# Silu against tanh for the expert tiles that run beside a selective scan, one Trainium2 core

## The chip, the core and the metric

The kernel runs on one core of a Trainium2 chip. A core has a matrix engine (TensorE, PE in the profile, with its weight loads as PEld), an elementwise engine (VectorE, DVE), an engine for activation functions (ScalarE, ACT), a third elementwise engine that here also starts the indirect transfers (GpSimd, POOL), and a queue that starts most of the other transfers (SyncE, SP). Each engine works through its own list of instructions strictly in order; they meet only in semaphores. An instruction that has to wait holds up everything behind it on its engine.

The metric is the device time of the whole program in microseconds (us), as the median of several executions. Profiles are of one execution each.

## The reference

The model is one Mamba block and one mixture of experts, each with a residual and a layer norm, over 4096 tokens of width 256 in float32. Cut to what matters:

```python
xz = x @ W_in.T;  x_in, z = split(xz)                  # 512 + 512 wide
u  = silu(causal_conv4(x_in) + b_conv)
dt = softplus(u @ W_dt.T + b_dt);  B, C = u @ W_B.T, u @ W_C.T
h[t] = exp(dt[t] * A) * h[t-1] + dt[t] * B[t] * u[t]   # 512 channels x 16 states
y[t] = sum_n h[t] * C[t]
x1 = layernorm(x + (y * silu(z)) @ W_out.T)

p = softmax(x1 @ router.T);  six best of 32 experts by p + bias, weights renormalised
gate, up = split(x1 @ gate_up[e].T)                    # 128 + 128, for each chosen expert e
routed = sum_e weight_e * ((silu(gate) * up) @ down[e].T)
shared = (silu(x1 @ sg.T) * (x1 @ su.T)) @ sd.T
out = layernorm(x1 + routed + shared)
```

The change touches `silu(gate) * up` of the routed experts, and only for about half of them.

## The kernel before

**Chunks and units.** The 4096 tokens are cut into eight chunks of 512. For each chunk and each of two halves of the channels, 16 states by two blocks of 128 channels are scanned: 64 units of 128 channels by 512 tokens a chunk, 512 in all. The loop over units (L1223) writes the instructions of all engines in program order. For unit q it issues

- on ScalarE `keep(q-1)` (L1159), which copies the last column of the state that unit q-1 has left, and `exp_at(q+2)` (L1132), the decay factors of the unit after next, into a tile `h` in PSUM that has three buffers. So the exponential for unit q+2 may start only when VectorE has done with unit q-1, and it has to be ready when VectorE comes to unit q+2;
- on GpSimd `du_at(q+4)` (L1121), the input term, four units ahead;
- on VectorE the scan itself (L1260), which reads `h` and `du` and writes `h`, and the product with C (L1267), which writes `hc`;
- on TensorE, three units later, the transposes (L1178) that sum `hc` over the states.

**What runs beside the scans.** Everything else is cut into Python generators, kept in a list `threads`; `step()` (L160), called once for each unit, advances each of them to its next `yield`, and whatever it issues takes its place in the engines' lists there. Nothing is moved afterwards. The generators are: `front(c+1)`, which projects, convolves and gates the next chunk and makes its step sizes (L867; its two long silu at L917 and L919, its logarithms at L971); `tail(c-1)` and `prepare`, which project the output of the chunk before, normalise it, route it and compute the shared expert (the square root of the norm at L181, a tanh for the shared gate at L367); `copies`, which scatter the routed rows into tiles of one expert each; and, from the third chunk on, the expert tiles.

**The expert tiles.** There are 224 tiles of 128 rows. They go in pairs. The 56 pairs of the first six chunks run as `pair` (L674) beside the scans of chunks 3 to 7, with weights loaded for them; the other 56 run as `through_all` (L1293) after the scans, with all experts' weights in SBUF. A `pair` waits for its rows, transposes them (L641), copies them back through ScalarE (L644, L647), multiplies with the gate and up weights into one PSUM bank `pg` (L682: gate in half 0, up in half 1), takes tanh of half the gate on ScalarE (L690), and one `yield` later, that is one unit later, makes `(tanh(g/2) + 1) * g` and its product with `up` on VectorE (L693, L694). Then come the down projection (L700), the weighting by ScalarE (L658) and an indirect add to memory by GpSimd (L664). `(tanh(g/2) + 1) * g` is twice silu(g); the row weights carry the factor one half.

**Function tables.** The profile shows the rows `ACT_TABLE_LOAD` on ScalarE, 1283 ns each, wherever the next function is not in the set that is loaded. The compiler places them directly ahead of the instruction that needs them. In the kernel before they stand ahead of the square root, the long silu, the logarithm, and ahead of the first exponential after each of these; none stands ahead of a tanh while exponentials run.

Of the kernel before, what the change touches and what calls it, by code (L numbers as in the profile page):

```python
# [10 lines left out]
AF = mybir.ActivationFunctionType  # L11
ALU = mybir.AluOpType
# [48 lines left out]
def kernel(  # L61
# [20 lines left out]
    nc = tc.nc  # L82
# [50 lines left out]
    def room():  # L133
        while held[0] >= len(pools):
            yield

    def bank(name):
        held[0] += 1
        turn[0] += 1
        return pools[turn[0] % len(pools)].tile([P, T], F32, tag="mm", name=name)  # L140

    def free():
        held[0] -= 1
# [4 lines left out]
    def take(tag, n):  # L148
        while live.get(tag, 0) >= n:
            yield  # L150
        live[tag] = live.get(tag, 0) + 1

    def give(tag):
        live[tag] -= 1
# [479 lines left out]
    def turned_rows(j, xt):  # L634
        yield from take("xsT", 2)
        yield from room()
        pt = bank(f"pt_{j}")
        pt4 = pt.rearrange("p (i k t) -> p i k t", i=2, k=KD)
        for i in range(2):
            for k in range(KD):  # L640
                nc.tensor.transpose(pt4[:, i, k, :], xt[:, i, ts(k, P)], ident)  # L641
        yield
        xT = q2.tile([P, 2, KD, P], F32, tag="xsT", name=f"xsT_{j}")
        nc.scalar.copy(xT.rearrange("p i k t -> p (i k t)"), pt)  # L644
        free()
        no = q2.tile([P, 2], I32, tag="no", name=f"no_{j}", bufs=8)
        nc.scalar.copy(no, xt[:, :, D])  # L647
        turned_out.add(j)
        yield
        return xT, no  # L650

    def added(j, po, wt, no, behind):

        tag, n = ("ytl", 4) if behind else ("yt", 2)
        yield from take(tag, n)
        yt = (f3 if behind else q2).tile([P, 2, D], F32, tag=tag, name=f"{tag}_{j}", bufs=n)
        for i in range(2):
            nc.scalar.mul(yt[:, i, :], po[:, i, :], wt[:, i : i + 1])  # L658
        free()
        yield  # L660
        for i in range(2):
            yield
            apart_from[0] = False
            a = nc.gpsimd.indirect_dma_start(  # L664
                out=acc[(j + i) % LANES],
                out_offset=bass.IndirectOffsetOnAxis(ap=no[:, i : i + 1], axis=0),
                in_=yt[:, i, :],
                in_offset=None,
                compute_op=ALU.add,
            )  # L670
            adds.append(a.ins)
        give(tag)

    def pair(j, xt, wt, gu, dn):  # L674

        xT, no = yield from turned_rows(j, xt)
        yield from room()
        pg = bank(f"pg_{j}").rearrange("p (h i t) -> p h i t", h=2, i=2)
        for h in range(2):
            for i in range(2):  # L680
                for k in range(KD):
                    nc.tensor.matmul(  # L682
                        pg[:, h, i, :], gu[i][:, k, ts(h, P)], xT[:, i, k, :],
                        start=(k == 0), stop=(k == KD - 1),
                    )
        give("xsT")
        yield from take("hm", 2)
        yield
        gt = q2.tile([P, 2, P], F32, tag="gt", name=f"gt_{j}")
        nc.scalar.activation(gt, pg[:, 0, :, :], AF.Tanh, scale=0.5)  # L690
        yield
        hm = q2.tile([P, 2, P], F32, tag="hm", name=f"hm_{j}")
        nc.vector.scalar_tensor_tensor(gt, gt, 1.0, pg[:, 0, :, :], ALU.add, ALU.mult)  # L693
        nc.vector.tensor_mul(hm, gt, pg[:, 1, :, :])  # L694
        free()
        yield
        yield from room()
        po = bank(f"po_{j}").rearrange("p (i d) -> p i d", i=2)
        for i in range(2):
            nc.tensor.matmul(po[:, i, :], hm[:, i, :], dn[i], start=True, stop=True)  # L700
        give("hm")
        give("dn")
        yield
        yield from added(j, po, wt, no, False)
# [713 lines left out]
```

## Time and profile before

| | |
|---|---|
| time, median of 3 executions | 1851.69 us (1851.32 to 1852.23) |
| the profiled execution: its time, its span | 1859.8 us, 1857.9 us |
| granted TensorE clock, mean | 0.839 |
| scans, first to last start | 72.0 to 1507.0 us |
| tanh of the pairs (L690), first to last start | 602.4 to 1524.3 us |
| PE, DVE, ACT, POOL busy over the span | 73%, 75%, 53%, 65% |
| ACT_TABLE_LOAD rows of the exponential's line L1132 | 29, 37.2 us |

The span runs from the first to the last instruction of the profiled execution. A group's row gives the source line, the engine, the operation, its output and inputs with their shapes, the number of instructions, then the busy time in us and the mean ns of one, then the idle time of the engine directly ahead of them and what ended it. A row of waits reads "who waited, for whom: total us, how many times, longest us". A row of the timeline gives the start in us, the duration in us, engine, line, operation, and in brackets the idle time ahead of it.

### The profile page before, as it was taken

What the parts mean: (1) busy time and instruction counts of PE and PEld (TensorE: products, weight loads), DVE (VectorE), ACT (ScalarE), POOL (GpSimd) and SP (SyncE); (2) the same over time, 40 slices, a digit from 0 to 9 for tenths busy, and PEclk for the clock granted to TensorE, in tenths of its full rate; (3) what the DMA queues carried; (4) which work ended last, traced back from release to release, by engine and by line L of the source; (5) the groups of instructions that cost most, each with busy time, mean ns of one, the idle gap of its engine ahead of it and who ended that gap; (6) DMA issues with size and microseconds to landing.
All of it is one profiled execution on the core that took longest, in us unless ns stands there. A gap on an engine that the chain in (4) does not pass through costs nothing. (4 is left out here: it accounts for less than half of the span.)

```text
span 1857.9 us, 24110 instructions
## 1 busy us (share of the span) xinstructions
PE 1359.2 (73%) x6208; PEld 944.8 (51%) x6208; DVE 1399.4 (75%) x2328; ACT 990.9 (53%) x2131; POOL 1216.3 (65%) x961
## 2 busy tenths in 40 slices
PE   8585696588669866986699668967775668699940
PEld 4242453355345545653566456645654566477730
DVE  1689989998998899779987998799979854122217
ACT  3676464547445755475557465756552333355533
POOL 0455644774585569665886599658956874878863
PEclk9796697779769887988989888988886987799975
DMA  8443692673469667875989589858998996599879
GB/s 238 136 126 102 219 307 77 164 212 123 94 192 257 166 160 177 251 206 126 258 215 263 131 234 245 236 139 214 271 257 236 260 268 100 123 145 144 144 131 306
DMA packets 318121, 355.40 MB, mean 191 GB/s; under 512 B 65056, under 2 KB 245024, under 8 KB 317984
## 3 DMA queue, kind: packets, MB, share of 16 engines
q1 hardware_dynamic: 274400, 296.02, 56.7%
q0 software_dynamic: 41472, 57.80, 17.3%
q8 instruction: 51, 0.84, 0.2%
q14 instruction: 86, 0.70, 0.1%
q10 hardware_dynamic: 2112, 0.05, 0.1%
HBM read 244.97 MB, written 108.77 MB: 190 GB/s over the span
## 5 line engine op out<-in xcount | busy, mean ns | idle before, releaser
L1121 POOL TENSOR_TENSOR du<-wall,bb 128x512 f32<-128x512 f32 x512 | 694.9, 1390 | 417.5 <-DVE h L1260 216.8
L1260 DVE TENSOR_TENSOR_SCAN h<-h,hlast,du 128x512 f32<-128x512 f32 x512 | 657.1, 1283 | 52.2 <-ACT hlast L1159 27.3
L1178 PE MATMUL y<-ident,hc 128*128 128x128 f32 x2048 | 345.2, 311 | 124.0 <-DVE hc L1267 104.0
L1132 ACT ACTIVATE h<-wall,aneg 128x512 f32<-128x512 f32 x512 | 353.7, 692 | 95.0 <-DVE hc L1267 80.4
L1267 DVE TENSOR_TENSOR hc<-h,cb 128x512 f32<-128x512 f32 x512 | 354.3, 692 | 58.6 <-DMA cb<-bcd 14.2
L1178 PEld LDWEIGHTS y<-ident,hc 128*128 128x128 f32 x2048 | 278.6, 162 | 233.9 <-DVE hc L1267 136.3
L552 POOL DMA_INDIRECT xs<-row,at x192 | 192.3, 1001 | 72.5 <-issue 39.2
L664 POOL DMA_INDIRECT acc<-ytl,no x112 | 174.8, 1561 | 59.4 <-issue 32.9
L664 POOL DMA_INDIRECT acc<-yt,no x112 | 177.5, 1585 | 53.2 <-ACT yt L658 28.7
L1159 ACT COPY hlast<-h 128x1 f32<-128x1 f32 x448 | 70.9, 158 | 260.7 <-DVE hc L1267 260.4
L1310 DVE SCALAR_TENSOR_TENSOR gt<-gt,pg 128x256 f32<-128x256 f32 x56 | 23.6, 421 | 175.5 <-ACT gt L1308 175.5
L682 PE MATMUL pg<-xsT,gu 128*128 128x128 f32 x896 | 123.8, 297 | 31.5 <-ACT xsT L644 25.4
L682 PEld LDWEIGHTS pg<-xsT,gu 128*128 128x128 f32 x896 | 118.0, 210 | 46.8 <-ACT xsT L644 29.5
L700 PE MATMUL po<-dn,hm 128*128 128x256 f32 x224 | 75.6, 469 | 83.5 <-DVE hm L694 35.6
L941 PE MATMUL pd<-wall 128*128 128x512 f32 x256 | 127.9, 649 | 9.5 <-DVE key L469 4.2
L905 PE MATMUL pv<-wall 128*128 128x512 f32 x256 | 117.4, 602 | 5.9 <-ACT hlast L1159 3.2
L1301 PE MATMUL pg<-wall,xsT 128*128 x448 | 113.0, 398 | 1.0 <-ACT xsT L644 1.0
L700 PEld LDWEIGHTS po<-dn,hm 128*128 128x128 f32 x224 | 46.9, 228 | 102.2 <-DVE hm L694 33.5
L641 PE MATMUL pt<-ident,xt 128*128 128x128 f32 x448 | 76.7, 298 | 24.1 <-DMA xt<-xs 21.2
L1301 PEld LDWEIGHTS pg<-wall,xsT 128*128 128x128 f32 x448 | 85.1, 200 | 12.3 <-ACT xsT L644 2.1
L941 PEld LDWEIGHTS pd<-wall 128*128 128x128 f32 x256 | 51.6, 211 | 66.8 <-issue 60.6
L641 PEld LDWEIGHTS pt<-ident,xt 128*128 128x128 f32 x448 | 61.0, 155 | 41.9 <-issue 25.3
(192 smaller groups left out, 1929.0 us busy)
## 6 DMA issues: line engine op xcount, KB each, us to landing
bb<-bcd SPq DMA_DIRECT2D x256, 256.0 KB
cb<-bcd SPq DMA_DIRECT2D x256, 256.0 KB
xs<-blank SPq DMA_DIRECT2D x55, 578.0 KB
xt<-xs SPq DMA_DIRECT2D x224, 128.5 KB
gu<-in_gate_up_t_dram SPq DMA_DIRECT2D x112, 256.0 KB
dn<-in_down_t_dram SPq DMA_DIRECT2D x112, 128.0 KB
wall<-acc SPq DMA_DIRECT2D x24, 512.0 KB
acc<-blank SPq DMA_DIRECT2D x16, 512.0 KB
```

The source lines that it names most:

```text
L552: i = nc.gpsimd.indirect_dma_start(out=xs, out_offset=bass.IndirectOffsetOnAxis(ap=at[:, b, k : k + 1], axis=0), in_=row[:, b, :], in_offs ...
L641: nc.tensor.transpose(pt4[:, i, k, :], xt[:, i, ts(k, P)], ident)
L664: a = nc.gpsimd.indirect_dma_start(out=acc[(j + i) % LANES], out_offset=bass.IndirectOffsetOnAxis(ap=no[:, i : i + 1], axis=0), in_=yt[:, ...
L682: nc.tensor.matmul(pg[:, h, i, :], gu[i][:, k, ts(h, P)], xT[:, i, k, :], start=(k == 0), stop=(k == KD - 1),)
L700: nc.tensor.matmul(po[:, i, :], hm[:, i, :], dn[i], start=True, stop=True)
L941: nc.tensor.matmul(pd, w_dt[:, k, ts(m, P)], u[:, k, :], start=(k == 0), stop=(k == M - 1),)
L1121: nc.gpsimd.tensor_mul(parts(q, du), u, row_for(q, 0))
L1132: nc.scalar.activation(h[:, ts(i, Tc)], dt_of[c][:, m + i, :], AF.Exp, scale=aneg[:, m + i, n : n + 1],)
L1178: nc.tensor.matmul(y_of[c, g][b // 2][:, b % 2, ts(m + j - 2 * g, P)], hc[:, ts(j * nb + b, P)], ident, start=(opens and j == 0 and b % 2 ...
L1260: nc.vector.tensor_tensor_scan(h, h, du_of.pop(q), hlast[:, n, m : m + 1], ALU.mult, ALU.add)
L1267: nc.vector.tensor_mul(parts(q, hc), parts(q, h), row_for(q, 1))
L1301: nc.tensor.matmul(pg[:, i].rearrange("p h t -> p (h t)"), xT[:, i, k, :], w, start=(k == 0), stop=(k == KD - 1),)
```

## The change

The gate's activation in `pair` becomes silu instead of tanh of the half, and the first of the two VectorE instructions goes. The second is now a three-operand instruction that multiplies silu by 2 and by `up`; the factor 2 keeps the row weights as they are. `through_all` and the shared expert keep the tanh.

```diff
         gt = q2.tile([P, 2, P], F32, tag="gt", name=f"gt_{j}")
-        nc.scalar.activation(gt, pg[:, 0, :, :], AF.Tanh, scale=0.5)
+        nc.scalar.activation(gt, pg[:, 0, :, :], AF.Silu)
         yield
         hm = q2.tile([P, 2, P], F32, tag="hm", name=f"hm_{j}")
-        nc.vector.scalar_tensor_tensor(gt, gt, 1.0, pg[:, 0, :, :], ALU.add, ALU.mult)
-        nc.vector.tensor_mul(hm, gt, pg[:, 1, :, :])
+
+        nc.vector.scalar_tensor_tensor(hm, gt, 2.0, pg[:, 1, :, :], ALU.mult, ALU.mult)
         free()
         yield
```

In the instruction lists of the two programs every engine keeps its order. VectorE has 56 instructions fewer. ScalarE has 107 more, all of them table loads: 54 ahead of the silu at L690, and 53 ahead of an exponential at L1132. The typical sequence on ScalarE was: exponential, tanh, `keep`, exponential. It is now: exponential, load, silu, `keep`, load, exponential.

## The prediction

> **What bounds the kernel now.** I read the page first, then the waits, then the timelines of ScalarE and VectorE around single tiles.
>
> ```profile
> span 1857.9 us, 24110 instructions
> ...
> PE 1359.2 (73%) x6208; PEld 944.8 (51%) x6208; DVE 1399.4 (75%) x2328; ACT 990.9 (53%) x2131; POOL 1216.3 (65%) x961
> ...
> L1260 DVE TENSOR_TENSOR_SCAN h<-h,hlast,du 128x512 f32<-128x512 f32 x512 | 657.1, 1283 | 52.2 <-ACT hlast L1159 27.3
> ...
> L1267 DVE TENSOR_TENSOR hc<-h,cb 128x512 f32<-128x512 f32 x512 | 354.3, 692 | 58.6 <-DMA cb<-bcd 14.2
> ```
>
> The scan and its product alone are 1011 us of VectorE, and they lie between 72 and 1510 us. In stretches of 180 to 190 us between 600 and 1330 us VectorE is busy for 156 to 167 us, 87 or 88%. So in the scans VectorE is the engine nearest to being the bound; what it still waits for there stands in the waits, columns total us, times, longest:
>
> ```profile
> DVE gt L693 <- ACT gt L690: 34.5, 15, 5.8
> DVE h L1260 <- ACT hlast L1159: 27.3, 14, 5.0
> DVE h L1260 <- ACT h L1132: 18.4, 14, 3.8
> ...
> DVE hc L1267 <- DMA cb<-bcd: 14.2, 8, 3.2
> ```
>
> The reader sees two things. The largest waits of VectorE in this part end at ScalarE: 34.5 us at the tiles' activation, 45.7 us at exponentials and `keep`. And ScalarE as a whole is not full: 106.2, 105.2, 108.2 and 111.6 us busy in four stretches of 180, 180, 180 and 190 us, 59%. So what counts is where on ScalarE the new work falls.
>
> **What a load costs.** One that is there already, with its neighbours on ScalarE:
>
> ```profile
> 895.83 0.15 ACT L1159 COPY hlast<-h 128x1 f32<-128x1 f32 x1
> 896.00 1.28 ACT L1132 ACT_TABLE_LOAD   x1
> 897.29 0.69 ACT L1132 ACTIVATE h<-wall,aneg 128x512 f32<-128x512 f32 x1
> ```
>
> It starts 0.02 us after the copy has ended, and the exponential starts 0.01 us after it: nothing beside the 1.283 us. Without a load the next instruction starts some 0.06 us before the last has ended (exponential to tanh below: 911.50 against 911.44), so I take 1.36 us for each load. 107 of them by 1.283 are 137 us of busy ScalarE; 43 of the 56 pairs lie between 600 and 1330 us, and take its share there from 59% to (431 + 86 x 1.283) / 730 = 74%.
>
> The Trainium skill, "ScalarE: Activation LUTs", section "What ACT_TABLE_LOAD costs", gives the same 1283 ns and adds a drain of about 1380 ns to every switch, 2.66 us in all; its rules say to do all of one table set before switching, which speaks against this change. No drain shows in the rows above. By the page a pair's two loads would put 5.3 us ahead of an exponential that has 3.7 us to spare, 1.6 us late for 54 pairs, an estimate of 87 us more; by the row they fit.
>
> **The change part by part.**
>
> *Removed: 56 instructions at L693.* The timeline of a pair in a quiet place, VectorE:
>
> ```profile
> 914.48 0.41 DVE L693 SCALAR_TENSOR_TENSOR gt<-gt,pg 128x256 f32<-128x256 f32 x1
> 914.92 0.42 DVE L694 TENSOR_TENSOR hm<-gt,pg 128x256 f32<-128x256 f32 x1
> ...
> 917.19 1.28 DVE L1260 TENSOR_TENSOR_SCAN h<-h,hlast,du 128x512 f32<-128x512 f32 x1
> ```
>
> From start to start one instruction is 0.44 us. The new form of L694 is that of the old L693 (414 against 421 ns, means over 56): no difference. 56 by 0.44 is 24.6 us, the upper end; the lower is 0. From it I take off: 7 pairs after 1442 us (3.1 us), because there the chain that ended last runs through transfers and GpSimd and not VectorE:
>
> ```profile
> 1442.64 11.78 DMA order<-li
> 1454.48 6.54 DMA bb<-bcd
> ```
>
> and 7 pairs in dense stretches (3.1 us, below), where VectorE would only wait longer for ScalarE. Of the 18.4 us left I let a fifth go at waits that VectorE does not set (matrix products for `pg`, `cb` transfers): 14.7 us.
>
> *Swapped: tanh for silu.* A silu over 2048 columns is 1911 ns, a tanh over 512 is 586 ns; the line through both gives 365 ns at 256 columns, the tanh here has 377. Nothing either way.
>
> *Added: a load ahead of silu.* ScalarE in the same place:
>
> ```profile
> 910.81 0.69 ACT L1132 ACTIVATE h<-wall,aneg 128x512 f32<-128x512 f32 x1
> 911.44 0.36 ACT L690 ACTIVATE gt<-pg 128x256 f32<-128x256 f32 x1
> 912.61 0.16 ACT L1159 COPY hlast<-h 128x1 f32<-128x1 f32 x1 [0.81 <-DVE hc L1267]
> 912.80 0.69 ACT L1132 ACTIVATE h<-wall,aneg 128x512 f32<-128x512 f32 x1
> ```
>
> The load waits for nothing, so where ScalarE stands idle for `pg` (16.2 us over 43 pairs) it is hidden in part; else silu ends 1.36 us later. Queued behind it on ScalarE are `keep` and the exponentials; waiting for it is L694, which stands one unit later on VectorE. I set the new end of each silu against the old start of its L693. Quiet pairs have room: 911.80 + 1.36 = 913.16, and VectorE comes at 914.48. Of 56 pairs 35 have it. 15 already make VectorE wait; there the delay is what the idle ScalarE does not hide, between 0 and 1.40 us, in sum 7.2. Another 6 lack 0.15 to 1.40 us, in sum 3.8. Together 11.0 us; bounds 0 and 56 x 1.36 = 76.
>
> *Added: a load ahead of the next exponential.* It stands behind `keep`, which waits for VectorE, so ScalarE's idle time before `keep` doesn't hide it (in chunk 7, without `keep`, it does). The exponential that ends at 913.49 is read at 917.19: 3.70 us to spare. Both loads take 2.72, and the removed instruction brings the scan 0.44 nearer: 0.5 us are left. That is the usual case; the middle value of this margin over the pairs is 3.7 us, but 12 of 53 have under 2.7. Following the delay down ScalarE's list until an idle stretch swallows it, 9 pairs make something on VectorE late: by 1.67, 1.83, 1.44, 0.46, 2.25, 1.35, 0.76, 2.58 and 0.24 us, 12.6 in sum. Most of them stand shortly ahead of the long silu, where ScalarE has no idle time and already makes a scan wait:
>
> ```profile
> 1196.88 1.28 ACT L917 ACT_TABLE_LOAD   x1
> 1198.17 1.91 ACT L917 ACTIVATE wall<-wall 128x2048 f32<-128x2048 f32 x1
> ...
> 1203.82 0.69 ACT L1132 ACTIVATE h<-wall,aneg 128x512 f32<-128x512 f32 x1
> ```
>
> ```profile
> 1204.61 1.29 DVE L1260 TENSOR_TENSOR_SCAN h<-h,hlast,du 128x512 f32<-128x512 f32 x1 [4.96 <-ACT hlast L1159]
> ```
>
> With the first part they overlap: counting the larger of the two for each pair gives 16.9 us, adding both 23.6. I take 20.3. From below it is bounded by 0 (the existing pairs of loads around the logarithms, such as that at 896.00, make no scan wait), from above by both loads of all 49 pairs before 1442 us, 133 us. I take a value near the low end, since it comes from the rows of the very places.
>
> *Behind.* Nothing moves on SP, GpSimd or TensorE. Late on ScalarE is also what follows silu: copies of rows (L644) for TensorE and `yt` (L658) for GpSimd's adds. GpSimd is four units ahead and already waits 216.8 us for VectorE at L1121, so up to 2.7 us are covered; without that cover the input terms would be late by as much. The end after 1510 us starts with loads that wait for the scans, so it shifts as a whole.
>
> **Sum:** 20.3 - 14.7 = 5.6 us slower. The profiled execution took 1859.8 us (span 1857.9), 8.1 over the median of 1851.7; I put the difference on the median: 1857.3 us.
>
> **Rivals.**
> *Faster: ScalarE's slack holds.* For it speaks the 41% of idle ScalarE, and the loads at the logarithms. If the added waits are the 11.0 us at L694 alone and 21 us of the saving land, it is 10 us faster, 1842. It decides as soon as the added waits stay under what lands of 24.6 us. Against it: the dense stretches have no idle time to give.
> *Nothing that can be measured:* waits and saving both near 15 to 18 us, 1852. For it speaks that the two sums are so near each other; measuring this kernel can tell about 0.2%, 3.7 us.
> *Much slower: delays spread.* My sums hold the other engines still. In the long chains of `front` ScalarE and TensorE wait for each other (ACT L910 for PE L905: 99.5 us), and a load there delays a copy, a product and the next copy, with exponentials queued behind them. If half of the second loads land, 25 x 1.36 = 34 us, with the 11.0, less 14.7: 30 us slower, 1882. Against it: 53 of these loads lie mostly in quiet stretches.
> *Silu next to the long silu would need no load:* excluded, the list has 54 loads for 56 silu.
>
> **How the numbers follow.** Forecast 0.45 (own range 1854 to 1866, a small part of it within 0.2%), faster 0.22, nothing 0.18, much slower 0.15. Slower is 0.42 + 0.15 = 0.57, within 0.2% is 0.18 + 0.03 = 0.21, faster 0.22. The range leaves out about half of the faster case below 1843, and most of the much slower above 1875.
>
> **What the profile will show.** ACT_TABLE_LOAD x54 at L690 and x82 at L1132, 1283 ns each with no gap; DVE 2272 instructions; the wait of L694 on silu from 34.5 to about 45 us; the scan's two waits on ScalarE from 45.7 to about 57; quiet pairs as before without waits. I am wrong if a load shows a gap behind it (a drain), if scans wait in quiet pairs, or if VectorE's waits on ScalarE grow by less than 12 us.

## The result and the profile after

The changed kernel takes 1867.68 us (median of 4 executions, 1865.91 to 1868.41) against 1851.96 us of the kernel before beside it: a ratio of 1.0075, 95% interval 1.0060 to 1.0091. By the ratio it is 14 us slower (11 to 17), by the two medians 16. The forecast was slower, by 5.6 us: the direction holds, the size does not.

The page of the profiled execution, and from the groups of ScalarE its table loads:

```profile
span 1866.2 us, 24155 instructions
...
PE 1361.1 (73%) x6208; PEld 945.7 (51%) x6208; DVE 1381.5 (74%) x2272; ACT 1125.0 (60%) x2238; POOL 1216.5 (65%) x961
```

```profile
L1132 ACT ACT_TABLE_LOAD x82 | 105.2, 1283 | 1.4
L690 ACT ACT_TABLE_LOAD x54 | 69.3, 1283 | 6.2 <-PE pg L682 5.2
```

VectorE has its 56 instructions fewer and is busy for 17.9 us less; ScalarE has 107 loads more and is busy for 134 us more. Against the columns of before (1399.4, 990.9) nothing else moved in the sums. The last scan ends at 1522.5 us after the span's start, before at 1508.3, 14.2 us later; so the loss lies in the scans. What comes after them took 343.7 us, before 349.6; over the profiled executions of all the kernels told here it takes 340 to 351 us, high and low without regard to the loads, and the profiled execution of the kernel before was itself 8 us over its median.

The waits of VectorE, columns as before (who, for whom: total us, times, longest):

```profile
DVE hm L694 <- ACT gt L690: 48.5, 24, 6.5
...
DVE h L1260 <- ACT hlast L1159: 33.9, 17, 6.2
DVE h L1260 <- ACT h L1132: 25.9, 20, 4.2
...
DVE h L1260 <- POOL du L1121: 12.9, 13, 2.3
```

The last of these rows in the kernel before:

```profile
DVE h L1260 <- POOL du L1121: 5.6, 6, 1.9
```

The wait for silu grew from 34.5 to 48.5 us (3.0 more are put down to `keep`), the scans' waits for ScalarE from 45.7 to 59.8, and the scans' wait for GpSimd's input terms from 5.6 to 12.9.

A pair shortly ahead of the long silu that the prediction showed. First VectorE in the kernel before, then ScalarE and VectorE in the changed one:

```profile
1188.90 0.42 DVE L693 SCALAR_TENSOR_TENSOR gt<-gt,pg 128x256 f32<-128x256 f32 x1 [0.48 <-ACT gt L690]
```

```profile
1200.26 1.28 ACT L690 ACT_TABLE_LOAD   x1
1201.55 0.38 ACT L690 ACTIVATE gt<-pg 128x256 f32<-128x256 f32 x1
1201.83 0.15 ACT L1159 COPY hlast<-h 128x1 f32<-128x1 f32 x1
1202.01 1.28 ACT L1132 ACT_TABLE_LOAD   x1
1203.30 0.69 ACT L1132 ACTIVATE h<-wall,aneg 128x512 f32<-128x512 f32 x1
```

```profile
1201.97 0.42 DVE L694 SCALAR_TENSOR_TENSOR hm<-gt,pg 128x256 f32<-128x256 f32 x1 [1.87 <-ACT gt L690]
...
1221.18 1.29 DVE L1260 TENSOR_TENSOR_SCAN h<-h,hlast,du 128x512 f32<-128x512 f32 x1 [6.16 <-ACT hlast L1159]
```

The product waits 1.87 us, 1.39 more than before (0.48); the prediction had 1.36 there. The scan that waited 4.96 us for the block with the long silu now waits 6.16. A pair in a quiet place, again ScalarE and VectorE:

```profile
918.87 1.28 ACT L690 ACT_TABLE_LOAD   x1
920.17 0.38 ACT L690 ACTIVATE gt<-pg 128x256 f32<-128x256 f32 x1
920.45 0.15 ACT L1159 COPY hlast<-h 128x1 f32<-128x1 f32 x1
920.62 1.28 ACT L1132 ACT_TABLE_LOAD   x1
921.91 0.69 ACT L1132 ACTIVATE h<-wall,aneg 128x512 f32<-128x512 f32 x1
```

```profile
921.83 0.41 DVE L694 SCALAR_TENSOR_TENSOR hm<-gt,pg 128x256 f32<-128x256 f32 x1
922.16 1.28 DVE L1260 TENSOR_TENSOR_SCAN h<-h,hlast,du 128x512 f32<-128x512 f32 x1
```

Neither instruction of VectorE has a bracket: both loads are covered. In the rows of both pairs the next instruction follows a load 0.01 us later, and so it does behind 161 of the 173 loads of this kernel; behind the other 12 stands an instruction that waits for another engine. There is no drain.

So the loads behave as read. What has to be explained is why the sum came out two and a half to three times as large.

### The profile page after: what moved, and what is told of

Its sections match the earlier page's. It is cut to its first block, busy times and chain, and to the rows that moved or that the text cites. A ratio compares the mean times of both kernels' runs of the same rounds, so it can differ in the third digit from the quotient of the medians.

```text
span 1866.2 us, 24155 instructions
## 1 busy us (share of the span) xinstructions
PE 1361.1 (73%) x6208; PEld 945.7 (51%) x6208; DVE 1381.5 (74%) x2272; ACT 1125.0 (60%) x2238; POOL 1216.5 (65%) x961
## 5 line engine op out<-in xcount | busy, mean ns | idle before, releaser
L1260 DVE TENSOR_TENSOR_SCAN h<-h,hlast,du 128x512 f32<-128x512 f32 x512 | 657.1, 1283 | 73.5 <-ACT hlast L1159 33.9
L1178 PE MATMUL y<-ident,hc 128*128 128x128 f32 x2048 | 341.4, 309 | 117.6 <-DVE hc L1267 99.2
L1132 ACT ACTIVATE h<-wall,aneg 128x512 f32<-128x512 f32 x512 | 353.2, 691 | 69.9 <-DVE hc L1267 55.3
L682 PE MATMUL pg<-xsT,gu 128*128 128x128 f32 x896 | 130.9, 308 | 35.5 <-ACT xsT L644 27.3
L682 PEld LDWEIGHTS pg<-xsT,gu 128*128 128x128 f32 x896 | 125.2, 221 | 51.9 <-ACT xsT L644 33.1
L1132 ACT ACT_TABLE_LOAD x82 | 105.2, 1283 | 1.4
```

Source lines behind the costliest of these rows:

```text
L682: nc.tensor.matmul(pg[:, h, i, :], gu[i][:, k, ts(h, P)], xT[:, i, k, :], start=(k == 0), stop=(k == KD - 1),)
L1132: nc.scalar.activation(h[:, ts(i, Tc)], dt_of[c][:, m + i, :], AF.Exp, scale=aneg[:, m + i, n : n + 1],)
L1178: nc.tensor.matmul(y_of[c, g][b // 2][:, b % 2, ts(m + j - 2 * g, P)], hc[:, ts(j * nb + b, P)], ident, start=(opens and j == 0 and b % 2 ...
L1260: nc.vector.tensor_tensor_scan(h, h, du_of.pop(q), hlast[:, n, m : m + 1], ALU.mult, ALU.add)
```

## Experiments

Each kernel ran beside the kernel before, in the same job on the same chip; jobs fell on chips on which the kernel before took 1852 to 1861 us, so ratios are compared and not times. All 12 are told here. Theory A: VectorE's saving lands nearly whole, and the loads cost more than I summed. Theory B: the split of the prediction (14.7 saved, 30 lost) holds. Theory C: the saving lands nowhere, and the loads cost what the change lost.

### The two halves of the change

One instruction on VectorE, tanh kept:

```diff
-        nc.vector.scalar_tensor_tensor(gt, gt, 1.0, pg[:, 0, :, :], ALU.add, ALU.mult)
-        nc.vector.tensor_mul(hm, gt, pg[:, 1, :, :])
+        nc.vector.scalar_tensor_tensor(hm, gt, 2.0, pg[:, 1, :, :], ALU.mult, ALU.mult)
```

> The tanh and the lists of ScalarE stay as before, and VectorE has one instruction a pair instead of two (it multiplies twice the tanh by up; the sum with one and the product with the gate are left out, so this is only about time). Theory A, the saving of VectorE lands nearly whole and the loads cost more than I summed: 18 to 24 us faster than before, about 1831. Theory B, the split of the prediction (14.7 us land): 12 to 17 us faster, about 1837. Theory C, the saving is lost at waits that VectorE does not set, and the loads cost only what the change lost in all: within 4 us of before.

Measured: 0.9994 of before (0.9974 to 1.0015), between 5 us faster and 3 us slower.

Silu and its loads, two instructions on VectorE:

```diff
-        nc.scalar.activation(gt, pg[:, 0, :, :], AF.Tanh, scale=0.5)
+        nc.scalar.activation(gt, pg[:, 0, :, :], AF.Silu)
...
-        nc.vector.scalar_tensor_tensor(gt, gt, 1.0, pg[:, 0, :, :], ALU.add, ALU.mult)
-        nc.vector.tensor_mul(hm, gt, pg[:, 1, :, :])
+        nc.vector.scalar_tensor_tensor(gt, pg[:, 0, :, :], 0.0, gt, ALU.mult, ALU.add)
+        nc.vector.scalar_tensor_tensor(hm, gt, 2.0, pg[:, 1, :, :], ALU.mult, ALU.mult)
```

> Silu with all its loads, but VectorE keeps two instructions a pair (the first one passes silu on unchanged, in the form of the old first one). Theory A: 34 to 40 us slower than before, about 1889. Theory B: 28 to 33 us slower, about 1882. Theory C: 14 to 20 us slower, 1868, as the whole change. If the two halves do not add up to the change, one of them works through the other.

Measured: 1.0082 (1.0060 to 1.0104), 15 us slower (11 to 19). Theory C holds and A and B fall: the loads alone cost what the whole change costs, and taking 24.6 us from VectorE bought nothing that can be told, with the loads (1.0075 against 1.0082) or without them.

Where each half acts can be read from the starts of the scans. For each quarter of a chunk (16 units), the table gives how much longer it took than in the kernel before, summed over chunks 3 to 7; it is worked out from the timelines of one execution each, on different chips:

```
units of the chunk          0-16   16-32   32-48   48-64     sum
pairs in it (of before)        8      15      14      19
one vector instruction      +6.5    -2.8    -4.1    -1.8    -2.2
loads alone                 -1.2   +13.4    +0.1    +2.9   +15.1
the change                  +5.2   +13.9    -5.3    +0.6   +14.4
```

Three kernels told below show how far such a table can be trusted. The kernel before with one unit more takes the same time as before, and yet its row sums to +8.5 us: a few us in an entry say little. The loads behind the tanh have 19.9 of their 24.5 us in units 16 to 32 too, and the kernel with the second load ahead of `keep` 13.8 of 19.6. That last kernel has one vector instruction, and again +5.8 us in units 0 to 16; the loads behind the tanh go with two, and have -0.3 there.

The loads cost most of their time in units 16 to 32. That is where ScalarE is busiest and where the long silu stands; two of these stretches, and the two that follow them, in the kernel before (columns: stretch and its length, then the busy time of PE, PEld, DVE, ACT and POOL, the granted clock, the share of the DMA engines, GB/s):

```profile
983.10:1035.80 52.70, 44.21 (x220) 29.67 (x219) 46.28 (x84) 36.32 (x74) 36.66 (x28) 0.95 0.83 224
1035.80:1090.70 54.90, 39.41 (x181) 26.57 (x180) 52.55 (x105) 29.98 (x65) 39.84 (x34) 0.83 0.69 161
1090.70:1129.70 39.00, 25.54 (x157) 22.27 (x156) 36.35 (x45) 23.28 (x54) 34.66 (x29) 0.82 0.91 263
...
1173.90:1228.00 54.10, 46.99 (x228) 30.40 (x227) 44.67 (x85) 37.95 (x76) 32.75 (x26) 0.94 0.76 206
1228.00:1282.70 54.70, 38.81 (x169) 27.33 (x167) 52.44 (x105) 30.76 (x66) 39.44 (x33) 0.81 0.72 170
```

ScalarE is busy for 69 and 70% of the two stretches of units 16 to 32, and for 55 and 56% of those of units 32 to 48, where 14 pairs' loads cost 0.1 us in all.

The row of one vector instruction says where the saving may go: it comes in units 16 to 64, 8.7 us, and is given back in units 0 to 16 of the next chunk, 6.5 us. The surest part of the gain is in units 32 to 48, where VectorE is busy for 96% of both stretches shown (52.55 of 54.90 us, 52.44 of 54.70): there 14 pairs save 6.2 us by the forecast's 0.44 each, and both rows with one instruction gain 4 to 5. In units 16 to 32 it is busy for 88 and 83%. The waits of the kernel with one vector instruction, and VectorE and GpSimd around the start of a chunk:

```profile
DVE h L1259 <- ACT hlast L1158: 32.4, 15, 5.5
DVE hm L693 <- ACT gt L690: 29.0, 9, 5.8
...
DVE h L1259 <- ACT h L1131: 23.3, 17, 3.8
DVE h L1259 <- POOL du L1120: 16.8, 18, 2.3
```

```profile
946.45 1.29 DVE L1259 TENSOR_TENSOR_SCAN h<-h,hlast,du 128x512 f32<-128x512 f32 x1 [0.57 <-POOL du L1120]
...
950.82 1.29 DVE L1259 TENSOR_TENSOR_SCAN h<-h,hlast,du 128x512 f32<-128x512 f32 x1 [2.35 <-POOL du L1120]
```

```profile
943.51 1.61 POOL L664 DMA_INDIRECT acc<-yt,no  x1 [0.16 <-issue]
944.56 1.85 POOL L1120 TENSOR_TENSOR du<-wall,bb 128x512 f32<-128x512 f32 x1
946.58 1.00 POOL L552 DMA_INDIRECT xs<-row,at  x1 [0.17 <-issue]
947.89 1.59 POOL L664 DMA_INDIRECT acc<-yt,no  x1 [0.30 <-issue]
```

The scans' wait for GpSimd rose from 5.6 to 16.8 us, those for ScalarE from 45.7 to 55.7: together 21.2 us, about the VectorE work that was taken away. GpSimd issues scatters, adds and input terms here without a pause; in the stretch 1090.70 to 1129.70 above, units 48 to 64 of the kernel before, it is busy for 34.66 of 39.00 us. A VectorE that comes earlier finds GpSimd no earlier. With the loads alone, and two instructions on VectorE, this wait stays as it was before:

```profile
DVE h L1261 <- POOL du L1122: 5.6, 7, 1.8
```

### Is it GpSimd?

Three kernels leave out the second indirect add of each pair, 56 times 1.58 us on GpSimd:

```diff
         yield
+        if i and not behind:
+            continue
         apart_from[0] = False
```

The kernel before with it:

> Before, with the second of the two indirect adds of each pair left out (half of the rows of the pairs are not added, so this is only about time): 56 times 1.58 us less on GpSimd. It is the base for the next two. If GpSimd, whose list is full around the starts of chunks, sets part of the pace: 5 to 15 us faster than before, 0.992 to 0.997. If not: within 4 us.

Measured: 0.9855 (0.9834 to 0.9876), 27 us faster, twice what I had thought.

The kernel with one vector instruction and half of the adds:

> The same with one instruction a pair on VectorE (and the sum and the gate's product left out). If the gain of the one-instruction kernel was taken away by GpSimd, it lands now: 10 to 20 us faster than the kernel with half of the adds, 0.985 to 0.992 of before. If it was taken away elsewhere (ScalarE's and TensorE's chains ahead of the long silu): within 5 us of the kernel with half of the adds.

Measured: 0.9805 (0.9784 to 0.9826). Against the kernel with half of the adds that is 0.9949, with the two intervals put together about 0.992 to 0.998: 9 us faster, 4 to 15.

The changed kernel with half of the adds:

> The changed kernel, likewise with half of the adds left out. If GpSimd only took away the saving, and the loads cost 15 us by themselves: it is no more than 0 to 5 us slower than the kernel with half of the adds. If the loads cost as they did and the saving lands nowhere: 12 to 18 us slower than that kernel.

Measured: 0.9925 (0.9903 to 0.9948), 1.0071 of the kernel with half of the adds (about 1.004 to 1.010), 13 us slower, 7 to 19.

With GpSimd relieved the saving does land in part, about 9 of 24.6 us (4 to 15), where it was within 5 us of nothing. The quarter at the start of the chunk no longer gives it back: against the kernel with half of the adds, one vector instruction less gives -2.2, -1.7, -5.7 and -4.9 us in the four quarters. So the adds took part of the saving; as the two intervals meet near 4 to 5 us, that is likely and not certain. The adds left out also take transfers off the DMA engines, so that these runs cannot tell GpSimd's own time from the transfers that it starts. The change does not become harmless, as the first expectation had it: between the last two kernels the loads cost 1.012, some 22 us (17 to 28), perhaps more than the 15 (11 to 19) before. What takes the other 15 us of the saving is not shown. In the kernel with one vector instruction the scans' waits for ScalarE had risen by 10.0 us; between the two kernels with half of the adds they stay at 43.6, and the wait of the product with C for its transfer rises from 4.9 to 10.4.

The kernel before, complete, with more lead for GpSimd:

```diff
-        du = p3.tile([P, T], F32, tag="du", name=f"du_{q}", bufs=6)
+        du = p3.tile([P, T], F32, tag="du", name=f"du_{q}", bufs=7)
...
-            du_at(q + 4)
+            du_at(q + 5)
```

(and the fifth input term made ahead of the loop).

> Before, complete, with the input terms made five units ahead in seven buffers instead of four units ahead in six, so that GpSimd may run one unit further ahead before its list is full. If GpSimd's being late around the starts of chunks costs time in the kernel before: its 5.6 us of waits shrink, 3 to 8 us faster, 0.996 to 0.998. If GpSimd is held there by transfers of B or by VectorE itself: 0.999 to 1.001.

Measured: 1.0094 (1.0069 to 1.0119), 17 us slower; both expectations failed. GpSimd's waits in that kernel:

```profile
POOL du L1121 <- DMA bb<-bcd: 234.4, 84, 60.7
POOL du L1121 <- DVE h L1261: 157.9, 81, 6.5
```

In the kernel before, the first of these and the long first wait of the program, which is put down to another row there:

```profile
POOL du L1121 <- DMA bb<-bcd: 106.9, 42, 8.4
POOL du L1121 <- DVE wall L976: 60.7, 1, 60.7
```

So without that first wait of 60.7 us the waits for the rows of B grew from 106.9 to 173.7 us, while those for the scan fell from 216.8 to 157.9. The rows of B are loaded no earlier than they were, so GpSimd stands at an input term waiting for its row, and the scatters and adds stand behind it. That the adds and scatters held up in this way make the 17 us is argued. A lead would have to move the transfers too; that was not tried.

### Which wait costs

Loads behind the tanh, as a silu of one column on a spare tile:

```diff
         nc.scalar.activation(gt, pg[:, 0, :, :], AF.Tanh, scale=0.5)
+        nc.scalar.activation(spare[:, 1:2], spare[:, 0:1], AF.Silu)
```

> Before, with a silu of one column on a spare tile directly behind the tanh: the same 107 loads, but none ahead of the tanh, so that VectorE's pair of instructions gets its tanh as early as before; only keep and the exponentials come later. If the two waits are separate terms (theory A): the scans wait 14 us more for ScalarE and perhaps 4 for GpSimd, 15 to 20 us slower than before, about 1869, and the wait of L696 on tanh stays near 34.5 us. If it is the load ahead of silu that counts: under 6 us slower. If any 2.7 us on ScalarE cost the same wherever they stand: as slow as the loads alone, over 28 us.

Measured: 1.0141 (1.0121 to 1.0161), 26 us slower, and 1.006 of the loads alone (about 1.003 to 1.009). None of the three fits: its interval, 22 to 30 us, reaches the "over 28" of the last, but it is not as slow as the loads alone, it is slower. Keeping the load from the tanh made it worse, and VectorE's wait for the tanh did not stay at 34.5 us, it is 39.9. From the groups of ScalarE in this kernel:

```profile
L693 ACT ACT_TABLE_LOAD x54 | 69.3, 1283 | 1.0
...
L692 ACT ACTIVATE gt<-pg 128x256 f32<-128x256 f32 x56 | 21.1, 376 | 33.5 <-PE pg L684 33.5
...
L693 ACT ACTIVATE spare<-spare 128x1 f32<-128x1 f32 x56 | 11.3, 203 | 0.6
```

ScalarE stands idle for 33.5 us ahead of the tanh, waiting for `pg`. With the loads alone it stands idle there for 10.8 us (1.0 ahead of the load, 9.8 ahead of silu): a load ahead of an instruction that waits anyway fills that idle time. Behind the tanh it fills none, and the short silu add 11.3 us. That is the difference in the place of the load; that it makes up the 11 us between the two kernels is argued and not shown by itself.

The second load ahead of `keep` instead of behind it:

```diff
         nc.scalar.activation(gt, pg[:, 0, :, :], AF.Silu)
+        nc.scalar.activation(spare[:, 1:2], spare[:, 0:1], AF.Exp)
```

> The changed kernel with an exponential of one column on a spare tile directly behind silu: the second load now stands ahead of keep, where ScalarE often stands idle waiting for VectorE, instead of behind it (112 loads instead of 107, and 56 short exponentials of about 0.2 us). If the loads cost through the exponentials that come late: the scans' waits on ScalarE fall from 59.8 us towards the 45.7 of before, and it is 5 to 10 us faster than the change, 1.002 to 1.006 of before. If it is the time that ScalarE is busy that counts, wherever it stands: 1 to 3 us slower than the change, 1.008 to 1.010.

Measured: 1.0080 (1.0051 to 1.0109), as the change, and as the second expectation had it; of the first the interval takes in the upper end alone. Its waits:

```profile
DVE h L1263 <- ACT hlast L1162: 36.9, 18, 6.2
...
DVE h L1263 <- ACT h L1135: 22.9, 17, 4.4
```

The scans wait 59.8 us for ScalarE, to the tenth what they wait in the changed kernel; they did not fall towards 45.7. A likely reason, not shown by itself, is that where there is idle time ahead of `keep` the load was covered anyway, and where it costs, there is none to move it into.

One unit more between silu and the product, in the changed kernel:

```diff
         yield
+        yield
         hm = q2.tile([P, 2, P], F32, tag="hm", name=f"hm_{j}")
```

> The changed kernel with one more yield between silu and the product on VectorE, so that VectorE comes to it two units later instead of one. If silu's delay is what VectorE waits for: its wait on silu falls from 48.5 us to under 25, and the time to 1852 to 1860. If the silu waits come from matrix products that are late anyway: the wait moves with it or turns up at the down projection, and the time is 1864 or more.

Measured: 1.0057 (1.0039 to 1.0075). Against the change's 1.0075 (1.0060 to 1.0091), from another job, the intervals overlap: no gain that can be told. The wait on silu fell as the first expectation had it, the time did not. And the same edit in the kernel before:

> Before, with one more yield between tanh and VectorE's two instructions: VectorE comes to them two units after the tanh instead of one. VectorE's 34.5 us of waits on the tanh go. If these waits set the pace: 10 to 20 us faster, 0.990 to 0.995. If they only stand in for another pace (as the wait on silu seemed to with the changed kernel one unit later), they turn up at the exponentials or at GpSimd's input terms: 0.998 to 1.004.

Measured: 1.0000 (0.9983 to 1.0017), as the second expectation had it. The waits of the two kernels, first the changed one:

```profile
DVE h L1261 <- ACT h L1133: 47.8, 38, 4.3
...
DVE h L1261 <- ACT hlast L1160: 34.0, 21, 5.6
...
DVE h L1261 <- POOL du L1122: 19.5, 19, 2.3
DVE hm L695 <- ACT gt L690: 11.9, 5, 3.9
```

```profile
DVE h L1261 <- ACT h L1133: 33.3, 22, 3.9
DVE h L1261 <- ACT hlast L1160: 27.8, 19, 5.0
...
DVE h L1261 <- POOL du L1122: 11.6, 16, 2.3
DVE gt L694 <- ACT gt L690: 9.4, 3, 3.5
```

In the kernel before, the 34.5 us of waits on the tanh fell to 9.4 (and 6.6 more that the profile puts down to `keep`); 15.4 us came back at the scans' waits for ScalarE and 6.0 at GpSimd, 21.4 of some 18 to 25 that went. A wait of VectorE is not a cost of its own that can be taken off the time.

### Who sets the pace

A third instruction on VectorE, in the kernel before:

```diff
+        nc.vector.scalar_tensor_tensor(gt, pg[:, 0, :, :], 0.0, gt, ALU.mult, ALU.add)
         nc.vector.scalar_tensor_tensor(gt, gt, 1.0, pg[:, 0, :, :], ALU.add, ALU.mult)
```

> Before, with a third instruction a pair on VectorE, of the form of the first (it passes the tanh on unchanged): 56 times 0.44, 24.6 us more of VectorE. If VectorE has slack in these chunks because something else sets their pace (why taking one instruction away bought nothing): under 6 us slower, below 1.003. If VectorE does set the pace and the one-instruction kernel lost its gain to something that happens only when VectorE is early: 15 to 25 us slower, 1.008 to 1.013.

Measured: 1.0037 (1.0020 to 1.0053), 7 us slower (4 to 10), between the two expectations: of 24.6 us more, 7 are paid; of 24.6 us less, nothing is gained. VectorE is one limit among several, not the one.

One of the two weightings of a pair moved from ScalarE to VectorE:

```diff
-            nc.scalar.mul(yt[:, i, :], po[:, i, :], wt[:, i : i + 1])
+            if i or behind:
+                nc.scalar.mul(yt[:, i, :], po[:, i, :], wt[:, i : i + 1])
+            else:
+                nc.vector.tensor_scalar_mul(yt[:, i, :], po[:, i, :], wt[:, i : i + 1])
```

> Before, with one of the two weightings of each pair (0.47 us, 56 of them) moved from ScalarE to VectorE: 26 us less on ScalarE, about 24 us more on VectorE. Against the kernel with three instructions on VectorE it differs only in what ScalarE has less. If ScalarE's busy time sets the pace: 10 us or more faster than that kernel, and at least as fast as before, 0.995 to 1.000. If it does not: the same as that kernel within 4 us.

Measured: 1.0052 (1.0034 to 1.0069), the same as the kernel with three instructions. ScalarE was busy for 20 us less (990.4 to 970.5), not 26, and that bought nothing. It does not show that ScalarE's busy time is without effect, because the two kernels differ in one thing more: the weighting now makes VectorE wait for the down projection and its weights.

```profile
DVE yt L661 <- PE po L703: 13.9, 5, 6.2
...
DVE yt L661 <- DMA dn<-in_down_t_dram: 6.4, 2, 5.6
```

VectorE's waits for ScalarE at the tanh and the scans fell by 15.2 us (75.2 to 60.0), and these 20.3 came in their place.

No kernel that computes the reference was faster than the kernel before.

## Why the prediction was right and wrong

- **The price of a load: right.** 1283 ns for each of the 173, and 0.01 us to the next instruction wherever that does not wait. ScalarE's share between 600 and 1330 us came to 528.6 of 730 us, 72%, forecast 74%. The drain that the Trainium skill, "ScalarE: Activation LUTs", "What ACT_TABLE_LOAD costs", adds to a switch does not show in this trace.
- **Where the loads cost: right.** Quiet pairs cover both; the dense stretch ahead of the long silu covers neither. 13.4 of 15.1 us fall in the quarter in which it stands, by one execution each.
- **What the loads cost, 20.3 us: somewhat high.** Alone they cost 15 us (11 to 19). The waits themselves were put too low, not too high: silu from 34.5 to 48.5 where I had about 45, the scans on ScalarE from 45.7 to 59.8 where I had about 57. A sum of waits is not a time, as the kernels with one unit more showed.
- **What VectorE saves, 14.7 us landing: the step that failed.** It measured nothing, 5 us at most. I had taken off what I could see is lost, a quarter of the work, and a fifth for other waits; the bound of 0 was in the range and was the value. The reading behind it was that VectorE, busy for 87%, is nearest to being the bound, so that work taken from it is time. An engine that is busy for 87% of a stretch and waits for ScalarE, GpSimd, TensorE and transfers in the other 13% gains only where no other chain arrives at the same moment. That the adds are one such chain is likely from the kernels with half of them; where the rest went stays open.
- **GpSimd's cover: it held for the loads, and was not asked for the saving.** I argued that GpSimd waits 216.8 us for VectorE and runs four units ahead, so 2.7 us are covered. With the loads alone the scans wait 5.6 us for it, as before. The wait grew with one vector instruction, to 16.8 us alone and 12.9 in the change. Waits summed over the program do not say whether GpSimd could follow a VectorE that comes earlier: in the stretch of units 48 to 64 shown above it is busy for 89%.
- **The sum.** Forecast 20.3 - 14.7 = 5.6; measured 15 - 0. The loads were 5 us too high and the saving 15 too high; the second error gave the size, and the first hid a third of it. The measured time, 1867.7 us, lies just above my own range, 1854 to 1866; by the ratio it is 1865.6, at its upper edge.
- **The rivals.** The faster case needed the saving to land, and fell with it. The case within 0.2% needed waits and saving to cancel; the waits came near their 15 us, and there was no saving against them. Much slower, by half of the second loads on top, did not come.

## What to carry to other kernels

Cost an instruction that is taken away stretch by stretch, as one that is added: ask what else would arrive at the end of each stretch if this engine came earlier, and count no saving where another engine's list is full. Look at the other engines' busy time in the same stretch, not at their waits summed over the program. Here a table load went unseen where the reader of the next result was far behind, and in front of an instruction that waits anyway it filled idle time; it cost time where ScalarE had none to spare. And test the two halves of a trade alone: here the half that was meant to pay did nothing.

## What the runs showed of the hardware

A table load can itself stand behind a wait: four of the 54 ahead of silu waited, one for 1.6 and one for 3.3 us, and 5.2 us in the group's row above ended at `pg`. I had taken it that a load waits for nothing. And 56 indirect adds less made the kernel 27 us faster, half a microsecond each of the 1.58 us that their rows show on GpSimd, though GpSimd as a whole is busy for only 65% of the span; the transfers that go with them are in these 27 us too.
